# The order of 48 attention blocks in a four-layer graph network: batches in lanes of four, or staggered by three blocks with the last layer's pieces spread out

## The chip, the cores and the metric

The kernel runs on one core of one Trainium2 chip. The metric is device time in microseconds (us) from start to end of the program. Before the change three runs took 4299.87, 4303.16 and 4289.3 us, median 4299.87. The profiled execution spans 4307.9 us.

The engines go by their names in the profile: PE (TensorE, matrix products), PEld (its weight loads), DVE (VectorE), ACT (ScalarE), POOL (GpSimd), SP (SyncE, which here issues transfers).

## What is computed

Sixteen batches of 1024 nodes with 128 features pass four graph layers, all in float32, over one adjacency matrix of 1024 x 1024 that all batches share. The first three layers are attention with 8 heads of 16, then a feed-forward part; the fourth is a graph attention whose scores are a sum of two terms per node.

```python
# layers 0, 1, 2
Q, K, V = h @ Wq, h @ Wk, h @ Wv               # 8 heads of 16
scores = einsum('bnhd,bmhd->bhnm', Q, K) / 4
scores = where(adj == 0, -inf, scores)
attn_out = einsum('bhnm,bmhd->bnhd', softmax(scores), V)
x = layer_norm(h + (attn_out @ Wo + bo))
x = layer_norm(x + relu(x @ W1 + b1) @ W2 + b2)
# layer 3
h = x @ W
e = leaky_relu((h @ a_src)[:, :, None] + (h @ a_dst)[:, None, :], 0.2)
e = where(adj == 0, -inf, e)
y = einsum('bij,bjd->bid', softmax(e), h) + x
out = layer_norm(y)
```

## The kernel before

A block is the attention of one batch b in one layer l of the first three: 48 blocks. A block is 32 steps: two groups of four heads (g), two halves of the queries (qh), eight tiles of the keys (kt). Each step issues the scores, and the product with V of the step four earlier. What lies around the attention (projections of the next block, the feed-forward part of the block before, the fourth layer) is cut into pieces, and at most one piece that is due follows each step. TensorE's order of instructions is the order of this program; the other engines' order is chosen when the kernel is compiled, by priority.

```python
AHEAD = 4
BOTH_ON_DVE = (2, 5, 7)
TILES = {"w": 10, "x": LANES + 1, "last": 2}     # LANES = 4

def slot(dtype=F32):                              # two banks of PSUM each
    return psum.tile([P, N], dtype, tag="s", name="s", bufs=3)
def bank():
    return psum.tile([P, 512], F32, tag="t", name="t", bufs=1)
def e_tile():
    return work.tile([P, J, 512], F32, tag="e", name="e", bufs=6)

def score_step(step):
    ...
    for pp in range(2):                           # two heads each
        ps = slot()
        for r in range(2):
            nc.tensor.matmul(ps[...], k[...], q[...], start=True, stop=True)          # L390
        on_pool = pp == 0 and kt not in BOTH_ON_DVE
        if on_pool:
            nc.scalar.activation(ev, psv, AF.Exp, scale=HD ** -0.5)                   # L397
            nc.gpsimd.tensor_mul(ev, ev, m)                                           # L398
        else:
            nc.vector.tensor_add(ev, psv, m)                                          # L400
            nc.scalar.activation(ev, ev, AF.Exp, scale=HD ** -0.5)                    # L401
    return e

def av_step(step, e, acc, first, last):
    for j in range(J):
        nc.tensor.matmul(acc[...], v_bufs[...], e[:, j, :], start=first, stop=last)   # L407
```

A projection is eight pieces: two transposed halves of x (t0, L260), two products each for keys and queries (L352, split by ACT and DVE into two parts, L354 and L355), two halves of V (L279). What follows a block ("post") is eleven: `both` (transposes on DVE), two out-projections (L279), two transposed halves (`x1t`, L260), four ffn1 (L461), two ffn2 (L279); out-projection and ffn2 are each followed by sums and statistics on DVE and `normalise` on POOL. Each piece of the chain uses the one bank `t`.

The fourth layer of a batch is a chain of 15 pieces:

```python
def edges(u):                       # a quarter of the queries; 2 x 8 matmuls with 4 rows
    def run():
        e = s["e", u] = e_tile()...
        for c in range(2):
            ps = slot()
            ... nc.tensor.matmul(ps[...], h_rows[row, ...], g_rows[row, ...])         # L564
            nc.vector.scalar_tensor_tensor(e[:, c:NT:2, :], ps, 1.0, mask01[...],
                                           op0=OP.max, op1=OP.mult)                   # L567
def aggregate(u):                   # that quarter times the nodes' features
    def run():
        e, ps = s["e", u], bank()
        ... nc.tensor.matmul(ps[...], e[...], s["hd"][...])                           # L576
        ... # reciprocal, sum with x, statistics on DVE; every second: normalise on POOL
def end():                          # scale and shift on POOL, both halves to the output
    ...
# (steps to wait since the piece before, piece, buffers taken and given back)
return [(5, xt(0), "+w +last +w +w"), (1, xt(1), "+w"), (2, nodes(0, 3), ""), (2, nodes(3, 6), ""), (2, nodes(6, 8), "-w -w"),
        (2, rows_gh, ""), (8, edges(0), ""), (2, edges(1), ""), (1, aggregate(0), ""),
        (2, edges(2), ""), (1, aggregate(1), ""), (2, edges(3), ""), (1, aggregate(2), ""),
        (2, aggregate(3), ""), (4, end, "-x -last -w -w")]

blocks = [(b, l) for p in range(0, B, LANES) for l in range(L) for b in range(p, p + LANES)]
```

The scheduler takes the first chain whose next piece is due. `need` takes the pieces of a chain at once, due or not, when the next block cannot do without them:

```python
def piece():
    for chain in chains:
        if now[0] >= chain["due"] + chain["queue"][0][0] and take(chain):
            return
...
if at == 6:                         # step 6 of block m
    need(("post",) + (blocks[m + 1][0], blocks[m + 1][1] - 1) if blocks[m + 1][1] else
         ("fetch", blocks[m + 1][0]))
    put(proj_tasks(m + 1), ("proj", m + 1), first=True)
```

Of the kernel before, what the change touches and what calls it, by code (L numbers as in the profile page):

```python
# [18 lines left out]
P = 128  # L19
H = 8  # L20
HD = 16
# [5 lines left out]
FLOOR = -1e29  # L27
NEG_SLOPE = 0.2
SOON = 120
LANES = 4  # L30
AHEAD = 4
BOTH_ON_DVE = (2, 5, 7)
TILES = {"w": 10, "x": LANES + 1, "last": 2}
BLOCKED = -57344.0


# [70 lines left out]
def fast_path(ctx: ExitStack, tc: tile.TileContext, a: dict, out: bass.AP, flag):  # L107
    nc = tc.nc
    x_dram, adj = a["x"], a["adj"]
    B, N, D = x_dram.shape  # L110
    NT = N // P
    NH = N // 512
    L = 3
# [15 lines left out]
    def half_tile(name):  # L129

        return work.tile([P, 512], F32, tag="w", name=name, bufs=TILES["w"])

# [4 lines left out]
    def load_x(b):  # L137
        t = work.tile([P, NT, D], F32, tag="x", name="x", bufs=TILES["x"])
        nc.sync.dma_start(t, x_dram[b].rearrange("(t p) d -> p t d", p=P))
        return t  # L140

    assert B % LANES == 0 and NT == 8 and D == H * HD == P and N == 2 * 512
    state = {("x", 0): load_x(0)}
    W = [load_layer(nc, nc.sync, const, a, 0, ("Wq", "Wk"))]
    W[0].update(load_layer(nc, nc.scalar, const, a, 0, ("Wv", "bo")))
# [352 lines left out]
    def last_tasks(b):  # L498
# [3 lines left out]
        def xt(h):  # L502
            def run():
                w = W[L - 1]
                if h == 0:

                    s["col"] = work.tile([P, 4, NT], F32, tag="col", name="col", bufs=2)
                    s["hd"] = [work.tile([P, 4, D + 1], F32, tag="w", name="hd", bufs=TILES["w"]) for _ in range(2)]
                    s["n"] = with_stats(state["x", b])
                s["xT", h] = transpose_half("xT", state["x", b], h, w["ln2_gc"], w["ln2_bc"])  # L510
                if h == 1:
                    scale_shift(state["x", b], w["ln2_g"], ln2_b_last)
            return run

        def nodes(t0, t1):
            def run():
                col, ts = s["col"], slice(t0, t1)

                halves = [slice(max(t0, 4 * h), min(t1, 4 * h + 4)) for h in range(2)]
                halves = [(c, s["hd"][c.start // 4][:, c.start % 4:(c.stop - 1) % 4 + 1, :])  # L520
                          for c in halves if c.start < c.stop]
                ps = bank()
                for t in range(t0, t1):
                    nc.tensor.matmul(ps[:, (t - t0) * (D + 2):(t - t0 + 1) * (D + 2)],
                                     s["xT", t // 4][:, t % 4 * P:(t % 4 + 1) * P], w_nodes, start=True, stop=True)
                pv = ps[:, :(t1 - t0) * (D + 2)].rearrange("p (t d) -> p t d", d=D + 2)
                with soon():
                    nc.scalar.activation(col[:, 2, ts], pv[:, :, D + 1], AF.Exp, scale=NEG_SLOPE)
                    nc.scalar.activation(col[:, 0:2, ts].rearrange("p c t -> p t c"), pv[:, :, D:], AF.Exp,
                                         scale=1 - NEG_SLOPE)  # L530
                    for c, hd in halves:
                        nc.vector.tensor_mul(hd[:, :, :D], pv[:, c.start - t0:c.stop - t0, :D],
                                             col[:, 2, c, None].to_broadcast([P, c.stop - c.start, D]))
                for c, hd in halves:
                    nc.scalar.copy(hd[:, :, D], col[:, 2, c])
            return run
# [18 lines left out]
        def edges(u):  # L555
            def run():
                e = s["e", u] = e_tile().rearrange("p j (c q) -> p (j c) q", q=256)
                for c in range(2):

                    ps = slot()  # L560
                    for i in range(2):
                        for r in range(2):
                            row = slice(64 * r + g0, 64 * r + g0 + 4)
                            nc.tensor.matmul(ps[:, (2 * r + i) * 256:(2 * r + i + 1) * 256],  # L564
                                             h_rows[row, (2 * i + c) * P:(2 * i + c + 1) * P],
                                             g_rows[row, u * 256:(u + 1) * 256], start=True, stop=True)
                    nc.vector.scalar_tensor_tensor(e[:, c:NT:2, :], ps.rearrange("p (j q) -> p j q", q=256), 1.0,  # L567
                                                   mask01[:, c:NT:2, u * 256:(u + 1) * 256], op0=OP.max, op1=OP.mult)
            return run
# [21 lines left out]
        def end():  # L591
            y = s["n"][0]
            for h in range(2):
# [1 line left out]
                queue = nc.scalar if h and b == B - 1 else nc.sync  # L595
                queue.dma_start(out[b].rearrange("(t p) d -> p t d", p=P)[:, 4 * h:4 * h + 4], y[:, 4 * h:4 * h + 4, :])

        return [(5, xt(0), "+w +last +w +w"), (1, xt(1), "+w"), (2, nodes(0, 3), ""), (2, nodes(3, 6), ""), (2, nodes(6, 8), "-w -w"),
                (2, rows_gh, ""), (8, edges(0), ""), (2, edges(1), ""), (1, aggregate(0), ""),
                (2, edges(2), ""), (1, aggregate(1), ""), (2, edges(3), ""), (1, aggregate(2), ""),  # L600
                (2, aggregate(3), ""), (4, end, "-x -last -w -w")]

    blocks = [(b, l) for p in range(0, B, LANES) for l in range(L) for b in range(p, p + LANES)]
    chains = []
    done = {("fetch", b) for b in range(2)}
    now = [0]
    free = dict(TILES)  # L610
    free["x"] -= 2
# [361 lines left out]
```

## Time and profile before

| What | Value |
|---|---|
| median of three runs | 4299.87 us |
| span of the profiled execution | 4307.9 us |
| mean granted TensorE clock | 0.974 |
| blocks 4 to 15, 345.9 to 1406.5 us | 1060.6 us |
| blocks 16 to 27, 1406.5 to 2468.0 us | 1061.5 us |
| blocks 28 to 39, 2468.0 to 3523.2 us | 1055.2 us |

The page gives for each engine its busy time, then the span in 40 slices (a digit is the busy share in tenths), then groups of instructions by source line with their mean length. The view by stretches gives the busy time of each engine between two times, with the count of instructions in brackets, then the granted clock of TensorE (1.00 is full), the transfers' share and rate. The view in order of time gives start, length, engine, source line, operation and tiles, how many instructions are merged, and in square brackets how long the engine had been idle and whose result ended that. A busy PE is not PE at its peak: lengths of matmuls overlap, so here the time from start to start counts.

### The profile page before, as it was taken

Reading aid. Unit: us, or ns where it says so; the run is one execution under the profiler, and the core shown is the slowest. Engines: PE = TensorE matmul, PEld = TensorE weight load, DVE = VectorE, ACT = ScalarE, POOL = GpSimd, SP = SyncE. Lnnn points to the kernel's source line nnn. Section 1 sums busy time; section 2 is a strip of 40 time slices with the busy share of each in tenths; the row PEclk is TensorE's granted clock in tenths of the full one; section 3 lists DMA queues with packets and bytes.
Section 4 is the critical chain, followed back from the end, with each engine's and each line's share of the span. In section 5 each row is a group of like instructions: output and inputs, shape, how many; then the busy total and the mean of one; then the engine's idle time right before and its main releaser. Section 6 shows DMA issues by size and latency. Waiting matters only on the chain. (4 is left out here: it accounts for less than half of the span.)

```text
span 4307.9 us, 70734 instructions
## 1 busy us (share of the span) xinstructions
PE 4005.4 (93%) x26069; PEld 1631.7 (38%) x26069; DVE 3408.0 (79%) x5324; ACT 3408.3 (79%) x3961; POOL 3442.0 (80%) x3010
## 2 busy tenths in 40 slices
PE   7999999999999999999999999999999999999996
PEld 2333333344443333334444333333344433333445
DVE  6888878877777888877777787887777788888774
ACT  7898989866767988987676898997776689898660
POOL 4788888876779888887677988887777788888784
PEclk9999999999999999999999999999999999999997
DMA  5222122221111222121112222221211212221100
GB/s 145 64 60 54 49 57 59 58 52 50 43 50 47 60 59 52 49 58 50 50 43 57 56 51 53 60 59 40 60 46 45 64 40 60 59 55 44 45 21 17
DMA packets 126147, 230.77 MB, mean 54 GB/s; under 512 B 36705, under 2 KB 75617, under 8 KB 125793
## 3 DMA queue, kind: packets, MB, share of 16 engines
q1 hardware_dynamic: 122896, 225.14, 20.9%
q8 instruction: 209, 3.42, 0.3%
q10 hardware_dynamic: 2896, 1.01, 0.1%
q14 instruction: 146, 1.19, 0.1%
HBM read 15.54 MB, written 8.39 MB: 6 GB/s over the span
## 5 line engine op out<-in xcount | busy, mean ns | idle before, releaser
L400 DVE TENSOR_TENSOR e<-s,mask_add 128x1024 f32<-128x1024 f32 x2112 | 2503.1, 1212 | 505.6 <-PE s L390 393.0
L401 ACT ACTIVATE e<-e 128x1024 f32<-128x1024 f32 x2112 | 2194.4, 1060 | 428.9 <-DVE e L400 415.3
L398 POOL TENSOR_TENSOR e<-e,mask 128x1024 f32<-128x1024 f32 x960 | 2047.3, 2145 | 470.2 <-ACT e L397 454.2
L407 PE MATMUL acc<-e,v 128*17 128x512 f32 x12288 | 1645.0, 607 | 44.9 <-POOL e L398 32.0
L390 PE MATMUL s<-Wq,Wk 64*128 64x512 f32 x6144 | 1217.0, 461 | 126.5 <-ACT e L397 54.8
L397 ACT ACTIVATE e<-s 128x1024 f32<-128x1024 f32 x960 | 979.8, 1021 | 137.8 <-PE s L390 73.6
L390 PEld LDWEIGHTS s<-Wq,Wk 64*128 64x128 f32 x6144 | 500.6, 186 | 1036.9 <-DVE e L400 330.9
L407 PEld LDWEIGHTS acc<-e,v 128*17 128x17 f32 x12288 | 206.5, 95 | 559.7 <-issue 440.6
L310 POOL TENSOR_SCALAR x<-x,mv 128x128 f32<-128x128 f32 x896 | 389.2, 447 | 22.7
L314 POOL TENSOR_TENSOR x<-x,ln_g 128x1024 f32<-128x1024 f32 (+1 forms) x97 | 228.8, 2359 | 129.8 <-PE t L260 118.9
L576 PEld LDWEIGHTS t<-hd,e 128*128 128x128 f32 x2048 | 259.3, 208 | 67.2 <-issue 31.8
L576 PE MATMUL t<-hd,e 128*128 128x129 f32 x2048 | 271.4, 295 | 7.8 <-DVE x L582 3.5
L308 POOL TENSOR_TENSOR mv<-mv,half_neg 128x4 f32<-128x4 f32 x224 | 232.0, 1036 | 18.3
L298 DVE TENSOR_TENSOR x<-t,x 128x512 f32<-128x512 f32 x192 | 132.1, 688 | 123.3 <-PE t L279 118.9
L461 PE MATMUL t<-x1T,W 128*128 128x512 f32 x384 | 217.7, 649 | 5.1 <-DVE x L582 1.0
L279 PEld LDWEIGHTS t<-W,hT 128*128 128x128 f32 x1536 | 183.9, 196 | 88.0 <-ACT hT L463 35.8
L279 PE MATMUL t<-W,hT 128*128 128x128 f32 x1536 | 202.5, 286 | 3.4 <-DVE lo L355 2.4
L291 DVE BATCH_NORM_STATS2 st<-x 128x6 f32<-128x128 f32 x896 | 197.3, 279 | 2.7
L260 PE MATMUL t<-identf,x 128*128 128x128 f32 x896 | 151.8, 294 | 36.5 <-DVE lo L355 25.5
L260 PEld LDWEIGHTS t<-identf,x 128*128 128x128 f32 x896 | 97.1, 144 | 230.7 <-DVE lo L355 55.8
L306 POOL TENSOR_SCALAR mv<-mv 128x4 f32<-128x4 f32 x224 | 52.8, 236 | 140.0 <-DVE mv L293 101.8
L463 ACT ACTIVATE hT<-t,b 128x512 f32<-128x512 f32 x192 | 132.2, 688 | 40.8 <-PE t L461 40.0
(83 smaller groups left out, 2588.0 us busy)
## 6 DMA issues: line engine op xcount, KB each, us to landing
Wk<-hi SPq DMA_DIRECT2D x384, 128.0 KB
Wk<-lo SPq DMA_DIRECT2D x384, 128.0 KB
Wq<-hi SPq DMA_DIRECT2D x384, 128.0 KB
Wq<-lo SPq DMA_DIRECT2D x384, 128.0 KB
x<-in_x_dram SPq DMA_DIRECT2D x16, 512.0 KB
out_dram<-x SPq DMA_DIRECT2D x31, 256.0 KB
ai<-in_adj_dram SPq DMA_DIRECT2D x8, 512.0 KB
g_rows<-parts SPq DMA_DIRECT2D x124, 4.0 KB
```

The costliest lines, as they stand in the source:

```text
L260: nc.tensor.transpose(ps[:, t * P:(t + 1) * P], src[:, 4 * h + t, :], identf)
L279: nc.tensor.matmul(ps[:, t * P:(t + 1) * P], lhs[f][:, t * P:(t + 1) * P], rhs[f], start=(f == 0), stop=(f == len(lhs) - 1))
L308: nc.gpsimd.tensor_tensor(v, v, half_neg[:, ts], OP.pow)
L310: nc.gpsimd.tensor_scalar(z[:, t, :], z[:, t, :], mv[:, t, 0:1], mv[:, t, 1:2], op0=OP.add, op1=OP.mult)
L314: nc.gpsimd.tensor_mul(z, z, rows(gain, n))
L390: nc.tensor.matmul(ps[:, r * 512:(r + 1) * 512], k[64 * r:64 * r + 64, kt * P:(kt + 1) * P], q[64 * r:64 * r + 64, q0:q0 + 512], start=Tru ...
L397: nc.scalar.activation(ev, psv, AF.Exp, scale=HD ** -0.5)
L398: nc.gpsimd.tensor_mul(ev, ev, m)
L400: nc.vector.tensor_add(ev, psv, m)
L401: nc.scalar.activation(ev, ev, AF.Exp, scale=HD ** -0.5)
L407: nc.tensor.matmul(acc[j * SLOT:j * SLOT + HD + 1, :], v_bufs[m % 2][:, kt, 2 * j + g, :], e[:, j, :], start=first, stop=last)
L576: nc.tensor.matmul(ps[:, i * (D + 1):(i + 1) * (D + 1)], e[:, t, i * P:(i + 1) * P], s["hd"][t // 4][:, t % 4, :], start=(t == 0), stop=(t ...
```

## The change

Before, four batches go together: layer 0 of all four, layer 1 of all four, layer 2 of all four. So the fourth layers of four batches come due within some seven blocks, and the next five blocks have none. After, every third block begins a batch, whose layers 0, 1 and 2 are four blocks apart; the order in between is (b, 0), (b - 1, 1), (b - 2, 2). Batches 2 and 3 begin earlier to fill the start. Each fourth layer can then be spread over the three blocks until the next one: for all but the last four batches each edges piece is followed by its aggregate two steps later, and the next edges piece comes 16 steps after that. The count of buffers is the same.

```diff
-LANES = 4
-TILES = {"w": 10, "x": LANES + 1, "last": 2}
+TILES = {"w": 10, "x": 5, "last": 2}
...
-        return [(5, xt(0), "+w +last +w +w"), (1, xt(1), "+w"), (2, nodes(0, 3), ""), (2, nodes(3, 6), ""), (2, nodes(6, 8), "-w -w"),
-                (2, rows_gh, ""), (8, edges(0), ""), (2, edges(1), ""), (1, aggregate(0), ""),
-                (2, edges(2), ""), (1, aggregate(1), ""), (2, edges(3), ""), (1, aggregate(2), ""),
-                (2, aggregate(3), ""), (4, end, "-x -last -w -w")]
-    blocks = [(b, l) for p in range(0, B, LANES) for l in range(L) for b in range(p, p + LANES)]
+        wide = b < B - 4
+        tasks = [(5, xt(0), "+w +last +w +w"), (1, xt(1), "+w"), (3, nodes(0, 3), ""), (3, nodes(3, 6), ""),
+                 (3, nodes(6, 8), "-w -w"), (2, rows_gh, "")]
+        if wide:
+            for u in range(4):
+                tasks += [(16 if u else 10, edges(u), ""), (2, aggregate(u), "")]
+        else:
+            tasks += [(8, edges(0), ""), (2, edges(1), ""), (1, aggregate(0), ""), (2, edges(2), ""),
+                      (1, aggregate(1), ""), (2, edges(3), ""), (1, aggregate(2), ""), (2, aggregate(3), "")]
+        return tasks + [(4, end, "-x -last -w -w")]
+    early = {(2, 0): 3.5, (3, 0): 7.5}
+    blocks = sorted(((b, l) for b in range(B) for l in range(L)), key=lambda x: early.get(x, 3 * x[0] + 4 * x[1]))
```

More of the change, by code (lines that the diff above doesn't have):

```diff
@@ L140, in load_x @@
         return t
-    assert B % LANES == 0 and NT == 8 and D == H * HD == P and N == 2 * 512
+    assert B >= 4 and NT == 8 and D == H * HD == P and N == 2 * 512
     state = {("x", 0): load_x(0)}
```

## The prediction

> **What bounds the kernel now.** I read the page's busy times and its 40 slices first, then cut the span into the 48 blocks (a new block is 128 score matmuls further on), then looked at single steps.
>
> ```profile
> PE 4005.4 (93%) x26069; PEld 1631.7 (38%) x26069; DVE 3408.0 (79%) x5324; ACT 3408.3 (79%) x3961; POOL 3442.0 (80%) x3010
> ACT  7898989866767988987676898997776689898660
> PEclk9999999999999999999999999999999999999997
> ```
>
> TensorE is far ahead of the others on average; the ACT row breathes with the period of four batches (9s where only attention runs, 6s and 7s where the fourth layer is mixed in). The busy shares by stretch show the two regimes: a plain block (5,1), and a block that carries a fourth layer (5,0).
>
> ```profile
> core 0: us, PE busy (x) PEld busy (x) DVE busy (x) ACT busy (x) POOL busy (x), PEclk, DMA share, GB/s
> 1561.10:1638.90 77.80, 74.09 (x486) 26.43 (x482) 65.34 (x97) 70.05 (x80) 67.10 (x57) 1.00 0.22 55
> 1103.90:1213.30 109.40, 99.79 (x658) 47.44 (x657) 80.26 (x139) 71.39 (x89) 77.08 (x71) 0.94 0.19 49
> ```
>
> Plain: PE 74.1 of 77.8, ACT 70.1. Mixed: PE 99.8 of 109.4, DVE only 73%, ACT 65%. So PE is the nearest to full in both, and the others have room in both. How much of PE's busy time is real need shows where it runs without a wait, in the order of time:
>
> ```profile
> start us, us, engine line op out<-in xcount [idle before <-releaser]
> 1604.39 0.73 PE L390 MATMUL s<-Wq,Wk 64*128 64x512 f32 x4
> 1605.06 1.05 PE L407 MATMUL acc<-e,v 128*17 128x512 f32 x8
> 1606.04 1.16 PE L279 MATMUL t<-Wv,xT 128*128 128x128 f32 x8
> 1607.13 0.73 PE L390 MATMUL s<-Wq,Wk 64*128 64x512 f32 x4
> ```
>
> From start to start: scores 0.67, attention times V 0.98 to 0.99, a projection half 1.09. A step without a piece is 1.645 us. In the same way, from other unhindered steps: a transposed half (L260 x4) 0.59, a 512-column product (L461 or L352 x2) 1.06, ffn2 (L279 x16) 1.98, three node columns (L524 x6) 0.87, an edges piece (L564 x8) about 1.03, an aggregate (L576 x32) 3.775.
>
> Need of PE per block: 32 x 1.645 = 52.6; projections 2 x 0.59 + 4 x 1.06 + 2 x 1.09 = 7.6; post 2 x 1.09 + 2 x 0.59 + 4 x 1.06 + 2 x 1.98 = 11.6; together 71.8 us. A fourth layer: 2 x 0.59 + 2.3 + 0.2 + 4 x 1.03 + 4 x 3.775 = 22.9 us per batch. A plain block lasts 77.5, so it waits 5.7: about 3.2 in the steps without pieces (there DVE and ACT set the pace), about 2.5 where two pieces follow each other and the single bank `t` waits for DVE. Twelve blocks (four batches) from 345.9 to 1406.5 last 1060.6; their need is 12 x 71.8 + 4 x 22.9 = 953.2. So only 107 us, 8.9 per block, are anything but PE's own work, and 5.7 of those 8.9 are in plain blocks too.
>
> **Where the rest goes in mixed blocks.** The chain of order around an edges piece:
>
> ```profile
> 867.62 0.77 PE L564 MATMUL s<-g_rows,h_rows 4*128 4x256 f32 x8
> 869.03 0.50 PE L390 MATMUL s<-Wq,Wk 64*128 64x512 f32 x2 [0.63 <-DVE e L400]
> 870.16 0.56 PE L390 MATMUL s<-Wq,Wk 64*128 64x512 f32 x2 [0.63 <-DVE e L567]
> 870.65 1.91 PE L407 MATMUL acc<-e,v 128*17 128x512 f32 x8
> 872.48 4.49 PE L576 MATMUL t<-hd,e 128*128 128x129 f32 x32
> ```
>
> Edges takes two of the three score slots and 2 x 1.2 us of DVE (L567, 1205 ns), and PE waits twice for DVE. After that L407 takes 1.91 instead of 1.05: the clock is halved.
>
> ```profile
> core 0: us, PE busy (x), PEclk, DMA share, GB/s
> 867.10:870.50 3.40, 2.14 (x20) 0.99 0.00 0
> 870.50:873.90 3.40, 3.40 (x16) 0.50 0.00 0
> ```
>
> I compared all stretches of 3.41 us of the clock records: those in which matmuls other than the 4-row edges ones cover at most 0.54 of the time are followed by half clock, those over 0.58 are not. Of the 48 edges pieces before the last block, 27 are followed by such a stretch. The clock shares of blocks 9 to 15 give 5.1 + 1.7 + 5.1 + 6.8 + 3.4 + 1.7 = 23.8 us lost per four batches, 6.0 per batch. The third loss is GpSimd, when scale-and-shift, normalise and the end piece meet:
>
> ```profile
> 1202.90 1.91 PE L407 MATMUL acc<-e,v 128*17 128x512 f32 x8 [4.00 <-POOL e L398]
> ```
>
> [...]
>
> **The change part by part.** Nothing is removed: the same pieces, so the need stays 953.2 per four batches. What moves: (1) I walked the new order and gaps through the scheduler's code, piece by piece (for the old order that gives the trace's sequence). From block 15 to 42 three kinds of block repeat, with need 80.3 (two aggregates, one edges, end), 76.4 (nodes, one edges, one aggregate, four of post's pieces pushed out) and 81.6 (two edges, one aggregate, double ffn2): mean 79.4.
> (2) Waits of each kind, from the same pieces' waits in the old trace. First kind: block start 0.9, `t` bank 0.9 + 1.2, edges 0.8, aggregates 0.3, free end 1.0 less 0.2, and GpSimd 3.0, because the aggregate's normalise (3.3), x1's scale-shift (4.7), the end piece (5.1) and two normalises (6.6) all fall in steps 19 to 28: 7.9. Second kind 7.0 (the old block 11, alike, had 6.2). Third kind 6.0. Sum 20.9.
> (3) Half clock: four edges pieces per batch as before, 56% of them at about 1.9 us: 4.2, down from 6.0.
> So three blocks take 238.3 + 20.9 + 4.2 = 263.4, twelve 1053.6, against 1060.6, 1061.5 and 1055.2 before. Over 28 such blocks that is -13 us.
> (4) Freed: the two edges tiles held at once (waits of ACT and DVE for L407, 60 + 42 us in all) are now one; these engines are not the bound, so I count nothing.
> (5) The end: batch 15's second layer is now two blocks, not four, ahead of its third, so all 11 pieces of its post are forced in one row at step 6 of block 46. Down that chain each product waits for the one bank and for ACT or DVE, and once for GpSimd's normalise (3.2): some 25 us, 11.6 of it need: +15.
> (6) Tail: block 47 and what follows took 205 us; batch 13's three last aggregates and 13 us of mixed work leave it, but they filled gaps in a chain of latencies: -5 net after the work is counted where it went.
> Sum: 4300 - 13 + 15 - 5 = 4297. My waits are summed one by one, and pieces that fill formerly free steps hide some of them (over the first twelve blocks DVE, ACT and POOL are busy 848.7, 850.3 and 858.9 of 1060.6, a fifth of room); 1 us less per block over the 28 is the correction I choose: 4270.
>
> **Rivals.** (a) Interleaving works: PE's waits in free steps (3.2 per block) vanish because every block has about five more pieces, and edges no longer meet edges. For it: DVE and ACT are idle a quarter of the mixed blocks. Then waits with the half clock fall from 8.9 to 5.5 per block, about 110 us over the 33 blocks from 11 to 43: 4190. Against it: edges waits come from slots and DVE in the very step, not from neighbours. (b) The half clock spreads: edges alone, with wide gaps, in blocks that had clock 1.00; first edges of a batch in the old trace were hit as often as later ones. At 75% hits and 6.83 us stretches it is 8 per batch, +45: 4330. (c) GpSimd becomes a local bound in the first kind: 6 instead of 3 us, +28, about 4310.
>
> **Range and chances.** One us per block is 33 us; I trust the waits to 1.2 us per block, so 40 us, and the end to 15 us. 8 in 10: 4200 to 4335. Faster by over 2% means under 4214: 0.18. Slower by over 2%, over 4386: 0.04. Within: 0.78.
>
> **What would show it.** Blocks in the middle all near 86 to 88 us with PE busy 93 to 95%; the ACT row flat at 7 or 8; the clock's mean near 0.975, its dips one per two edges and spread over the whole span; PE waiting for POOL's L398 once in three blocks; a gap of some 15 us in block 46. I am wrong if the middle blocks last under 84 (rival a), if the mean clock leaves 0.97 to 0.98, or if block 46 costs over 30 us.

## The result, and the profile after

| | before | after |
|---|---|---|
| median of four runs, us | 4301.51 (4289.3 to 4308.17) | 4363.77 (4362.34 to 4372.53) |
| span of the profiled execution, us | 4307.9 | 4370.6 |
| mean granted TensorE clock | 0.974 | 0.972 |

The changed kernel takes 1.0152 times as long, with a 95% interval of 1.0125 to 1.0179. The prediction, 4270 us in a range of 4200 to 4335, is missed by 94 us, on the slow side. From here on spans of the profiled executions are taken apart; their difference, 62.7 us, agrees with that of the medians, 62.3.

The page of the kernel after, busy times and ACT's row of the 40 slices:

```profile
PE 4011.6 (92%) x26069; PEld 1618.1 (37%) x26069; DVE 3402.5 (78%) x5324; ACT 3405.3 (78%) x3961; POOL 3443.5 (79%) x3010
...
ACT  7898988777878777787877878788787877868670
```

The count of PE's instructions is the same 26069, and ACT's row is as flat as the change meant it to be: 7 and 8 from the sixth slice to the thirty-fifth. The work is spread, and the kernel is slower all the same.

Three blocks in a row from the middle, (8,0), (7,1) and (6,2), in the view by stretches of the kernel after:

```profile
1814.10:1902.90 88.80, 83.75 (x556) 34.43 (x552) 70.22 (x115) 69.74 (x78) 70.23 (x61) 0.98 0.22 55
1902.90:1989.40 86.50, 80.48 (x519) 29.96 (x515) 68.87 (x94) 72.42 (x92) 68.87 (x49) 0.98 0.21 52
1989.40:2083.70 94.30, 86.34 (x563) 35.65 (x562) 72.50 (x125) 70.22 (x79) 75.78 (x79) 0.96 0.19 48
```

The first number after the times is the length, the last but two the clock. With the needs that the prediction gave to the three kinds (80.3, 76.4, 81.6), 8.5, 10.1 and 12.7 us of these blocks are something else. The whole kernel can be cut in the same way. For each stretch I count PE's pieces in the trace, price each at its length from start to start (the prediction's own figures), take half of the time that the clock records show at half speed as "half clock", and call the rest "wait". (Where PE also waits inside a stretch at half speed, this counts some wait as half clock. In blocks 16 to 39 of the two kernels that is under 2 us; in block 46 after the change it is 4 of the 17.1, behind it some 10 of the 30.)

| stretch | need before, after | wait + half clock before | after |
|---|---|---|---|
| blocks 0 to 15 | 1232.4, 1209.5 | 143.4 + 30.7 = 174.1 | 132.5 + 22.1 = 154.6 |
| blocks 16 to 39 | 1906.6, 1906.6 | 165.7 + 44.4 = 210.1 | 195.3 + 44.4 = 239.7 |
| blocks 40 to 45 | 432.0, 477.8 | 33.7 + 0 = 33.7 | 47.8 + 6.8 = 54.6 |
| block 46 | 88.3, 93.5 | 8.3 + 6.8 = 15.1 | 18.9 + 17.1 = 36.0 |
| block 47 and what follows | 153.9, 125.8 | 32.5 + 29.1 = 61.6 | 42.4 + 30.1 = 72.5 |
| sum | 3813.2, 3813.2 | 383.6 + 111.0 = 494.6 | 436.9 + 120.5 = 557.4 |

The need is the same to a tenth; the change adds 53 us of wait and 9.5 of half clock. The gain at the start (19.5) and the loss in blocks 40 to 45 (20.9) go with the work of the fourth layers: 22.9 us of need have left the start, and 45.8 have come to blocks 40 to 45. What remains is **the middle, 30 us; block 46, 21; the tail, 11.**

How sure are these two columns? The mean clock is on record for every execution, so its half clock can be had as span x (1 - clock), to some 2 us. In 43 executions of the kernel before this is 94 to 116 us, mean 105, while the remainder of the span stays between 4188 and 4197: what differs from one execution to the next is the half clock. In the four of the kernel after it is 109 to 122, mean 113, and the remainder 4248 to 4252. The two that are taken apart here lie at the upper end, with 111 and 121. So a wait can be compared from one trace to another; a difference of half clock under some 20 us needs the other executions too.

**The middle.** Which waits these are, the view of what PE waits for says directly. Columns: the waiting operation's tile and line, what it waits for, us in total, times, longest. Blocks 16 to 39 before, then after (line numbers are one lower there: L389 is scores, L406 attention times V, L259 a transposed half, L278 out-projection, V or ffn2, L523 and L539 the fourth layer's nodes):

```profile
PE s L390 <- ACT e L397: 27.1, 57, 1.4
PE s L390 <- DVE e L400: 20.0, 32, 1.7
PE acc L407 <- POOL e L398: 20.0, 15, 4.0
PE t L279 <- DVE lo L355: 15.2, 22, 1.0
PE s L390 <- DVE e L567: 15.2, 22, 1.2
PE t L260 <- DVE lo L355: 12.2, 16, 1.0
```

```profile
PE t L278 <- DVE lo L354: 21.0, 24, 1.4
PE t L259 <- DVE x L297: 19.5, 8, 2.5
PE s L389 <- DVE e L566: 19.0, 32, 0.6
PE acc L406 <- POOL e L397: 17.0, 10, 2.1
PE s L389 <- DVE e L399: 15.2, 40, 0.5
PE s L389 <- ACT e L396: 14.1, 32, 0.5
```

Scores waited 62.3 us (27.1 + 20.0 + 15.2) and now wait 48.3: filling free steps does hide waits, 14 us of them. But pieces that wait for the bank `t` until DVE has split a projection (`lo`) go from 30.9 us (15.2 + 12.2, and 3.5 below the lines shown) to 45.9 (21.0 shown, and below the lines shown L523 with 8.8, L259 with 8.6 and L539 with 7.5): a node piece now stands between two projection products, where the bank is still full. And one group is new: eight times 2.4 us for `x L297`, once in every third block. GpSimd's own group hardly shrinks; it is in one place per three blocks now.

**The new wait, step 7 of the third kind.** PE, GpSimd and DVE of the kernel after, in order of time:

```profile
2011.53 0.66 PE L259 MATMUL t<-identf,x 128*128 128x128 f32 x4 [2.44 <-DVE x L297]
```

```profile
2002.26 1.74 POOL L309 TENSOR_SCALAR x<-x,mv 128x128 f32<-128x128 f32 x4
2003.96 4.24 POOL L397 TENSOR_TENSOR e<-e,mask 128x1024 f32<-128x1024 f32 x2
2008.16 0.61 POOL L420 TENSOR_TENSOR A<-tt,recs 128x256 f32<-128x256 f32 x1
```

```profile
2008.81 0.71 DVE L433 STREAM_TRANSPOSE aT<-A 128x512 f32<-128x512 f32 x1 [2.85 <-POOL A L420]
```

The ffn2 pieces of (8,0)'s post are pushed over the block's edge into steps 0 and 1. Their two normalises (L309, the second is shown) land on GpSimd just where it should make masks; it makes two masks, then `A`, the attention output divided by its sums. DVE, idle for 2.85 us, transposes it (aT), and only after that adds `x` to the out-projection (L297, at 2010.79), which frees the bank. The wait is followed by half clock: the attention product at 2013.09 takes 1.80, not 1.05.

**GpSimd, step 26 of the first kind.** GpSimd and PE of the kernel after:

```profile
1876.86 1.29 POOL L313 TENSOR_TENSOR x<-x,ln_gamma 128x512 f32<-128x512 f32 x1
...
1881.93 2.37 POOL L314 TENSOR_TENSOR x<-x,b 128x1024 f32<-128x1024 f32 x1
```

```profile
1886.44 1.45 PE L406 MATMUL acc<-e,v 128*17 128x512 f32 x8 [1.76 <-POOL e L397]
```

The end piece's scale and shift (`ln_gamma`, `ln_beta`) meets the scale and shift of x1 (`ln_g`, `b`); no mask is made from 1873.2 to 1884.2, and PE waits 1.76. Half clock follows: the next ffn1 takes 2.08, unhindered 1.06 to 1.12.

**Block 46.** Two of the eleven pieces in one row, the transposed halves, kernel after:

```profile
4064.05 1.76 PE L259 MATMUL t<-identf,x 128*128 128x128 f32 x4 [1.41 <-POOL x L309]
4067.61 1.76 PE L259 MATMUL t<-identf,x 128*128 128x128 f32 x4 [1.80 <-POOL x L309]
```

The whole row goes from 4057.8 to 4088.2, 30.4 us for 11.6 of need. A wait stands before every one of its ten products, 0.8 us at the least, 2.1 at the most; and all but the last run at half clock (a transposed half unhindered is 0.59 to 0.66, here 1.76). The waits in brackets sum to 10.9; the other 7.9 of the 18.8 us over the need are the slower clock.

### The profile page after: what moved, and what is told of

The parts are those of the page before. It is cut to its first block, busy times and chain, and to the rows that moved or that the text cites. A ratio compares the mean times of both kernels' runs of the same rounds, so it can differ in the third digit from the quotient of the medians.

```text
span 4370.6 us, 70636 instructions
## 1 busy us (share of the span) xinstructions
PE 4011.6 (92%) x26069; PEld 1618.1 (37%) x26069; DVE 3402.5 (78%) x5324; ACT 3405.3 (78%) x3961; POOL 3443.5 (79%) x3010
## 3 DMA queue, kind: packets, MB, share of 16 engines
q10 hardware_dynamic: 2896, 1.01, 0.1%
## 5 line engine op out<-in xcount | busy, mean ns | idle before, releaser
L397 POOL TENSOR_TENSOR e<-e,mask 128x1024 f32<-128x1024 f32 x960 | 2046.3, 2144 | 567.9 <-ACT e L396 565.9
L406 PE MATMUL acc<-e,v 128*17 128x512 f32 x12288 | 1645.9, 608 | 49.1 <-POOL e L397 27.9
L389 PE MATMUL s<-Wq,Wk 64*128 64x512 f32 x6144 | 1216.1, 461 | 108.8 <-ACT e L396 34.8
L389 PEld LDWEIGHTS s<-Wq,Wk 64*128 64x128 f32 x6144 | 500.8, 187 | 1031.9 <-DVE e L399 357.4
L406 PEld LDWEIGHTS acc<-e,v 128*17 128x17 f32 x12288 | 206.9, 96 | 567.4 <-issue 447.7
L309 POOL TENSOR_SCALAR x<-x,mv 128x128 f32<-128x128 f32 x896 | 389.2, 448 | 24.0
L313 POOL TENSOR_TENSOR x<-x,ln_g 128x1024 f32<-128x1024 f32 x97 | 228.7, 2357 | 46.7 <-PE t L259 39.6
L575 PEld LDWEIGHTS t<-hd,e 128*128 128x128 f32 x2048 | 240.2, 195 | 55.9 <-issue 19.7
L575 PE MATMUL t<-hd,e 128*128 128x129 f32 x2048 | 252.4, 282 | 3.2 <-DVE x L581 1.7
L297 DVE TENSOR_TENSOR x<-t,x 128x512 f32<-128x512 f32 x192 | 132.3, 689 | 152.0 <-PE t L278 146.1
L460 PE MATMUL t<-x1T,W 128*128 128x512 f32 x384 | 236.7, 701 | 5.9 <-ACT hT L462 3.1
L278 PEld LDWEIGHTS t<-W,hT 128*128 128x128 f32 x1536 | 183.0, 195 | 86.3 <-ACT hT L462 41.2
L259 PE MATMUL t<-identf,x 128*128 128x128 f32 x896 | 157.6, 297 | 59.9 <-DVE x L297 22.8
L278 PE MATMUL t<-W,hT 128*128 128x128 f32 x1536 | 201.4, 286 | 4.0 <-ACT hT L462 2.3
L290 DVE BATCH_NORM_STATS2 st<-x 128x6 f32<-128x128 f32 x896 | 196.2, 278 | 2.7
L259 PEld LDWEIGHTS t<-identf,x 128*128 128x128 f32 x896 | 98.6, 145 | 259.9 <-DVE x L297 50.9
```

The lines of the kernel that those rows point to most:

```text
L259: nc.tensor.transpose(ps[:, t * P:(t + 1) * P], src[:, 4 * h + t, :], identf)
L278: nc.tensor.matmul(ps[:, t * P:(t + 1) * P], lhs[f][:, t * P:(t + 1) * P], rhs[f], start=(f == 0), stop=(f == len(lhs) - 1))
L309: nc.gpsimd.tensor_scalar(z[:, t, :], z[:, t, :], mv[:, t, 0:1], mv[:, t, 1:2], op0=OP.add, op1=OP.mult)
L389: nc.tensor.matmul(ps[:, r * 512:(r + 1) * 512], k[64 * r:64 * r + 64, kt * P:(kt + 1) * P], q[64 * r:64 * r + 64, q0:q0 + 512], start=Tru ...
L406: nc.tensor.matmul(acc[j * SLOT:j * SLOT + HD + 1, :], v_bufs[m % 2][:, kt, 2 * j + g, :], e[:, j, :], start=first, stop=last)
L460: nc.tensor.matmul(ps, w["W1"][:, f * P:(f + 1) * P], s["x1T", h], start=True, stop=True)
```

## The experiments

Each expectation is quoted as it was written before the run. The time is the median, the ratio is to the kernel before on the same chip, with its 95% interval. "Middle" is wait + half clock of blocks 16 to 39, whose need is 1906.6 in every kernel but one (e15_early, 1907.8; the expectations price it at 1916 and so speak of 230 and 200 us for after and before); before has 165.7 + 44.4, after 195.3 + 44.4. Edits are to the kernel after, where nothing else is said.

**Order alone.** The new order with the old, dense gaps of the fourth layer:

```diff
-        wide = b < B - 4
+        wide = False
```

> The new order of blocks, with the old dense gaps for every batch. If the spreading of the edges pieces is what costs (they meet the half clock and the bank of the projections more often), the three-block cycle falls from 269 to about 264 us and the kernel takes about 4315. If the place of the other pieces costs (feed-forward pieces pushed into the next block, the end piece beside the scale-shift), it stays, since the dense pieces push them too: 4350 to 4380. The forced row in block 46 is the same in both.

4350.93 us, 1.0128 (1.0111 to 1.0145). Middle 187.4 + 25.6 = 213.0, against 210.1 before: without the spread, the staggered order leaves the middle's sum as it was, with more wait and less half clock. Its loss is the end: 52.5 in blocks 40 to 45, 34.8 in block 46, 72.6 after it, much as after. So in these two executions 27 of the 30 us of the middle belong to the spread, and the end to the order. That is an upper end: this execution was the fastest of its four, that of after the slowest, and over all executions the spread costs 10 to 13 us in all (ratio 1.0152 against 1.0128, median 4363.77 against 4350.93), the order some 50 of the 62. The waits of the middle are surer. With the dense gaps the scores wait 73.8 us (48.3 with the spread), the waits for the masks (L397) are 1.5 (17.0), those for `x L297` nil (19.5), those for `lo` 42.4 (45.9). The spread hides 25 us of the scores' waits and pays 35 on the two paths over GpSimd that are shown above; most of the added waits for `lo` came with the order.

**The forced row.** Batch 15's first layer two places earlier and its second one, so that the second is three blocks ahead of the third:

```diff
-    early = {(2, 0): 3.5, (3, 0): 7.5}
+    early = {(2, 0): 3.5, (3, 0): 7.5, (15, 0): 42.5, (15, 1): 46.5}
```

> The kernel after, but batch 15 begins two blocks earlier, so that its layers stand three blocks apart and no row of eleven pieces is forced in block 46. If the forced row and the cold clock behind it cost what block 46 shows (35.6 us of waits and half clock against 14.9 before), the kernel falls by 20 to 25 us, to about 4340. If the row's work only moved (a tail with more left to do), it stays at 4355 to 4370.

4350.63 us, 1.0123 (1.0104 to 1.0143). Block 46 has 5.6 + 0 of wait and half clock instead of 18.9 + 17.1: the row was worth 30.4. But 16 of it come back in the middle (204.7 + 51.2), most of it for a reason that is the experiment's own, in block 39:

```profile
3465.10 1.09 PE L259 MATMUL t<-identf,x 128*128 128x128 f32 x4 [12.00 <-DMA x<-in_x_dram]
```

Batch 15's input is now wanted too soon after its buffer comes free.

**Order of the pieces.** A piece of the fourth layer only when no other piece is due:

```diff
+    def only_last(chain):
+        mark = chain["queue"][-1][3]
+        return mark is not None and mark[0] == "last" and len(chain["queue"]) <= 15
...
-        for chain in chains:
+        for chain in sorted(chains, key=only_last):
```

> The kernel after, but a piece of the fourth layer is taken only when no piece of a feed-forward chain is due. If the pushed ffn2 pieces are a cause (block (6,2) waits 2.4 us for the out-projection's addition on VectorE, which waits for GpSimd, and the half clock follows), the cycle of three blocks loses 4 to 7 us and the kernel 40 to 65: about 4310. If the half clock behind edges alone is the cause, it changes by less than 15 us.

4387.02 us, 1.021 (1.0193 to 1.0227). The waits of the middle fall to 168.6, the level of before: post's pieces are no longer pushed over the edge of the block and node pieces leave the projections alone, though step 7 of the first kind now waits 1.7. The half clock rises to 54.6 (146 us in all over four executions, 113 in after), and in block 11 PE waits 11.7 us for a batch's input (blocks 0 to 15: 181.8 instead of 154.6). So these waits come from the places; mending the places alone does not mend the total.

**No fourth-layer piece in steps 9 to 18**, where the projections are (`only_last` as in the run before):

```diff
+            if only_last(chain) and 9 <= now[0] % 32 <= 18 and now[0] < 32 * len(blocks):
+                continue
```

> The kernel after, but no piece of the fourth layer is taken in steps 9 to 18 of a block, where the products of the next block's projections lie. If pieces between two such products wait for the single bank t (0.8 to 1.1 us each in the second kind: steps 10, 12, 14, 16), the waits of the second kind fall from 8.4 to about 6, and the cycle by 2 to 3 us: 4335 to 4345. If the waits only move to where the pieces go, it stays within 10 us of 4364.

4375.5 us, 1.0185 (1.0154 to 1.0216). Middle 179.1 + 47.8: 16 us of wait less. This is not the price of the node pieces alone: the waits for `lo` fall from 45.9 to 24.6 and those for `x L297` (19.5) go, while PE waits 39.0 instead of 17.0 for the masks and 66.2 instead of 48.3 at the scores. What is kept back lands elsewhere: 12.7 us more than after in blocks 0 to 15, and twelve aggregates instead of eight after block 46 (78.5 there, with 28.8 in block 46 itself).

**The end piece's share of GpSimd.** The last scale and shift is left out (gains are ones and shifts zeros in these inputs, but it is work left out: 5.1 us of GpSimd per batch):

```diff
-                scale_shift(y[:, 4 * h:4 * h + 4, :], wl["ln_gamma"], wl["ln_beta"])
```

> The kernel after without the last layer's scale and shift on GpSimd (5.1 us per batch left out, the gain being all ones and the shift all zeros in this data). If the end piece and x1's scale and shift, one behind the other on GpSimd, hold up TensorE in the first kind of block (1.8 us and the half clock behind it, 1.7), the cycle of three loses about 3.4 us, the kernel 35 to 50 us: about 4320. If GpSimd's load there is hidden, it stays within 10 us of 4364.

4326.24 us, 1.006 (1.004 to 1.008). Middle 180.0 + 25.6: 15 us of wait and 19 of half clock less. PE's waits for the masks (L397) in blocks 16 to 39 go from 17.0 to this:

```profile
PE acc L406 <- POOL e L397: 1.4, 8, 0.2
```

In this pair of executions more than half of what the meeting on GpSimd costs comes as half clock. Over all executions, and the whole span, it is less: the half clock falls by 15 us (113 to 99), the remainder of the span by 25 (4250 to 4225).

**Edges in halves**, two steps instead of one, so that one score slot is taken at a time:

```diff
-                tasks += [(16 if u else 10, edges(u), ""), (2, aggregate(u), "")]
+                tasks += [(16 if u else 10, edges(u, (0,)), ""), (1, edges(u, (1,)), ""), (1, aggregate(u), "")]
```

> The kernel after, but each edges piece of the first twelve batches is taken in two halves, one score slot and one VectorE operation each, in two steps after one another. If the two slots and 2.4 us of VectorE in one step are what stops TensorE and starts the half clock, the waits for L566 and the half-clock stretches behind edges go: 5 to 8 us per batch, the kernel at about 4280 to 4310. If VectorE's work is the cost wherever it lies, it stays within 15 us of 4364.

4345.88 us, 1.0118 (1.0099 to 1.0136). Middle 197.3 + 18.8. Edges pieces that half clock follows: 2 of 52 instead of 20; waits stay.

**Full matmuls added to edges.** Each edges piece gets four transposes of 128 x 128 whose result is never read; this is 0.59 us of added work per piece, 38 us in all 64:

```diff
                     ps = slot()
+                    for k in range(4 if c else 0):
+                        nc.tensor.transpose(ps[:, k * P:(k + 1) * P], w_nodes[:, :D], identf)
```

> The kernel after, with four more 128x128 transposes per edges piece, written into the second score slot ahead of the piece's own matmuls and never read: extra work of TensorE of 0.59 us, 64 times, 38 us. If the half clock comes from a 3.41 us stretch with too few matmuls of full height, the added ones lift such a stretch from 0.43 to 0.60 and the half clock behind edges goes: of 87.8 us lost in the first 47 blocks some 35 go, and the kernel stays within 20 us of 4364 though it does more. If the half clock comes from something else in an edges step (the wait itself), nothing goes and the kernel takes about 4395.

4350.03 us, 1.012 (1.0092 to 1.0148). Middle 196.0 + 27.3, where the added 19 us are counted as wait: they fit into time in which PE waited anyway, and 17 us of half clock go. Edges pieces that half clock follows: 9 of 52. The border that the prediction read from the trace of before (half clock up to 0.54 of a stretch covered, none over 0.58) does not carry over. It was not sharp in the trace of before: there a stretch covered to 0.547 (at 49 us) is followed by half clock, and one covered to 0.525 (at 4240 us) is not. Counted in the same way, both outcomes occur between 0.51 and 0.58 in the trace of after, and eight stretches with added transposes are covered to 0.606 to 0.609 here, and seven of them are followed by half clock.

**The same two, in the order of before.** To the kernel before, edges in halves, each quarter followed at once by its aggregate (all batches; then the first 13), and the added transposes in the first 13 batches:

```diff
-                    for k in range(4 if c else 0):
+                    for k in range(4 if c and b < 13 else 0):
```

> The kernel before, with its order and its bunched fourth layers, but each edges piece in two halves, one score slot each, followed by its aggregate. If the double piece causes the half clock in the mixed blocks (23.8 us of four batches), most of it goes: 15 to 20 us per four batches, the kernel at 4225 to 4250, faster than both. If bunching itself is the cause, it stays within 15 us of 4300.

> The kernel before, with halved edges pieces for batches 0 to 12 alone, the last three whole as they were. If the loss of the run with all batches halved lay only behind block 47 (264 us there against 216), the gain up to block 47 (15 us) now remains: 4280 to 4290. If halving costs elsewhere too, it stays at 4300 or above.

> The kernel before, with the four added transposes of 0.59 us in the edges pieces of batches 0 to 12 (52 times, 31 us of added work). If half clock follows a stretch with too few full matmuls and the transposes fill time in which TensorE waits anyway, half clock in blocks 8 to 39 falls from 68 us to 25 to 40 and the kernel is faster in spite of more work: 4265 to 4290. If the added work is not hidden, 4300 to 4325.

| | median, us | ratio | middle | after block 46 |
|---|---|---|---|---|
| before_split | 4343.39 | 1.0105 (1.0077 to 1.0133) | 179.4 + 27.3 | 106.6 |
| before_split12 | 4312.37 | 1.0027 (1.0015 to 1.004) | 180.6 + 25.6 | 80.7 |
| before_warm12 | 4259.77 | 0.9909 (0.9892 to 0.9925) | 167.1 + 15.4 | 57.4 |

Halves trade half clock for wait, and hurt the end, where the fourth layers are all that is left. The added transposes beat both kernels. The page's busy times, and the added transposes of one edges piece (L562) with the scores that follow, in this kernel:

```profile
PE 3988.5 (94%) x26277; PEld 1628.2 (38%) x26277; DVE 3405.0 (80%) x5324; ACT 3407.0 (80%) x3961; POOL 3442.6 (81%) x3010
```

```profile
859.73 0.66 PE L562 MATMUL s<-identf,w_nodes 128*128 128x128 f32 x4
...
861.45 0.49 PE L390 MATMUL s<-Wq,Wk 64*128 64x512 f32 x2 [0.20 <-DVE e L569]
```

208 instructions more, and PE is busy 17 us less than before (3988.5, was 4005.4), since fewer of the others run at half clock: 111.0 us lost to it before, 59.7 now, of the 53.4 by which the span is shorter. Over the executions on record the half clock is 61 us, where the kernel before on that chip has 106, and the remainder of the span 4197, against 4193. The piece that the prediction showed waits 0.63 for DVE, this one 0.20. The 52 x 0.59 = 31 us of added work are counted as wait here, and the waits of the middle are still 167.1, before 165.7: the added work lies in time in which PE waited anyway.

**A tidy spread.** Edges in halves, gaps of 4 and 1 steps (2 between node pieces), no piece in steps 9 to 18, the fourth layer last among those due, batch 15 earlier; and the same with whole edges:

```diff
-                tasks += [(16 if u else 10, edges(u), ""), (2, aggregate(u), "")]
+                tasks += [(4 if u else 8, edges(u, (0,)), ""), (1, edges(u, (1,)), ""), (1, aggregate(u), "")]
...
+            if only_last(chain) and len(chain["queue"]) > 1 and 9 <= now[0] % 32 <= 18 and now[0] < 32 * len(blocks):
+                continue
```

> All that the single runs point to, on the new order: a piece of the fourth layer only when no feed-forward piece is due and not in steps 9 to 18 (the end piece may), the edges pieces of the first twelve batches in halves with short gaps, and batch 15 begun one block earlier so that nothing is forced near the end. If the cost of the kernel after is where its pieces land, blocks 16 to 39, which hold the same work in every version (1916 us of TensorE's need), fall from 230 us of waits and half clock to 165 to 185 (200 before the change), and the kernel to 4270 to 4300. If mixing a fourth layer into every block costs by itself, blocks 16 to 39 stay over 205 us and the kernel over 4315.

> As the run before, but with whole edges pieces followed by their aggregate two steps later. If whole edges bring the half clock wherever they lie, blocks 16 to 39 have 15 to 30 us more of it than with halves, and the kernel takes 4290 to 4320; if place decides, it is within 8 us of the one with halves.

4414.8 us, 1.028 (1.0253 to 1.0307), and 4374.43, 1.0168 (1.0151 to 1.0185). Middle 209.1 + 70.0 and 189.3 + 61.4: the worst of both terms. An aggregate or half of edges at the start of a block meets the same path through GpSimd's `A`, now in two blocks out of three (step 7 of blocks 24 and 25 waits 2.40 and 2.61). Neither expectation of the second run held: with whole pieces the kernel has less half clock than with halves, and takes 40 us less. A free step is not a free place.

**The path through A.** Its product on DVE instead of GpSimd, in four kernels: after, tidy, after with the transposes and batch 15 earlier, and before_warm12:

```diff
-            nc.gpsimd.tensor_mul(state["A"][:, qh, :, g, :], tt[:, :, :HD],
+            nc.vector.tensor_mul(state["A"][:, qh, :, g, :], tt[:, :, :HD],
```

> The kernel after, with the product of the attention and its reciprocal sums (A) on VectorE in place of GpSimd. If the path from a busy GpSimd over A to the out-projection carries the loss, the wait of 2.4 us at step 7 of every third block and the half clock behind it (1.7) go: blocks 16 to 39 fall from 230 to 190 to 205 us of waits and half clock, the kernel to 4325 to 4345. If VectorE's added work (192 times some 0.3 us) sets back the scores as much, it stays at 4355 to 4375.

> The tidy run with A on VectorE. There the wait at step 7 or 10 stands in all three kinds of block (2.5, 2.5 and 3.7 us, each with the half clock behind it). If the path carries it, some 12 us per three blocks go, 100 over the kernel: 4300 to 4325. If the pieces' places cost by themselves, it stays above 4380.

> The kernel after with three mendings: the added transposes against the half clock, batch 15 begun one block earlier, A on VectorE. If the causes add up, 4364 less 14, 15 to 25 and 25 to 35 gives 4290 to 4310: no better than the kernel before without any. If the new order hides something more, it stays over 4320.

> The kernel before with the added transposes, and A on VectorE. If GpSimd's path also costs in the old order (waits of 4.0 us for the masked scores once in four batches, and three forced transposes), it falls from 4260 to 4240 to 4255; if VectorE's added work costs more than that, 4260 to 4275.

| | median, us | ratio | middle |
|---|---|---|---|
| after_A_dve | 4502.55 | 1.0478 (1.0449 to 1.0507) | 237.4 + 47.8 |
| tidy_A_dve | 4513.39 | 1.0499 (1.0465 to 1.0534) | 256.2 + 71.7 |
| after_warm_end_A | 4469.45 | 1.0395 (1.0365 to 1.0424) | 238.8 + 39.2 |
| before_warm12_A | 4418.29 | 1.0287 (1.0254 to 1.0319) | 228.5 + 41.0 |

All lose, in plain blocks too (blocks 17 to 19: 77.5 us before, 80.1 in before_warm12_A, without half clock in either). The product itself shows why; lengths are min, median and max in ns, before and in after_A_dve:

```profile
L421 POOL TENSOR_TENSOR A<-tt,recs x192: 611/622/647, 68.6 to 4200.4; 128x256 f32<-128x256 f32 x192
```

```profile
L420 DVE TENSOR_TENSOR A<-tt,recs x192: 403/1364/6233, 66.2 to 4402.6; 128x256 f32<-128x256 f32 x192
```

On DVE it can take 0.40 (the expectation's "some 0.3 us" was an estimate of mine, which no trace shows), and takes 1.36 in the middle case and up to 6.2. The long ones go with GpSimd's instructions. In after_A_dve 76 of the 192 products take 0.40 to 0.43 us. The other 116 take 0.61 or more; each of them begins while a GpSimd instruction runs, and ends 0.28 to 0.29 us after one has ended. One of them, with GpSimd's instruction:

```profile
158.94 2.39 POOL L313 TENSOR_TENSOR x<-x,ln_g 128x1024 f32<-128x1024 f32 x1 [3.00 <-PE t L259]
159.44 2.17 DVE L420 TENSOR_TENSOR A<-tt,recs 128x256 f32<-128x256 f32 x1
```

GpSimd ends at 161.33, the product at 161.61. What ties the two together, no run here shows. One more thing the run settles: in block 23 the wait at step 7 goes from 2.44 to none with no half clock after it, and the group `x L297` is gone from the waits of the middle. So the path is the one read above. Its worth could not be had this way.

**A sooner on GpSimd.** The product stays there and gets a higher priority:

```diff
+            with soon():
                 nc.vector.reciprocal(rec, tt[:, :, HD])
                 nc.gpsimd.tensor_mul(state["A"][:, qh, :, g, :], tt[:, :, :HD],
```

> The changed kernel, with the reciprocal and GpSimd's product of A put ahead in priority, nothing else. Theory (GpSimd's order makes the wait at step 7 of every third block): about 2.4 us of wait and 1.7 us of half clock go from one block in three; blocks 16 to 39 go from 230 us over their need to about 200, the kernel to 4325 to 4345. Rival (what GpSimd does first is not decided by priority there, or the wait only moves to the masks of the scores): 4355 to 4375.

4400.43 us, 1.0236 (1.0215 to 1.0258). The rival held: in the same place of this kernel GpSimd still makes both masks first,

```profile
2005.94 4.24 POOL L397 TENSOR_TENSOR e<-e,mask 128x1024 f32<-128x1024 f32 x2
2010.15 0.61 POOL L421 TENSOR_TENSOR A<-tt,recs 128x256 f32<-128x256 f32 x1
```

and the wait is 2.44 as before. Elsewhere the order did change: PE waits 22.8 us for the masks in the middle, it was 17.0. But 4400 is outside the rival's 4355 to 4375 too, and how is worth more than the run was meant to tell: the waits of the middle are those of after (196.2, was 195.3), and the half clock is 66.6 instead of 44.4. Of the 27.5 us between the two spans, 23.3 are half clock; over all executions it is 141 to 150 us, against 109 to 122 in after.

**The causes together**: transposes in all edges pieces, batch 15's first two layers one place earlier each (43.5 and 46.5, so that its input isn't late), A sooner:

> The changed kernel with the added transposes in each edges piece of the first thirteen or so batches, batch 15's first two layers two places earlier, and A's product put ahead on GpSimd. Theory: the three causes add up, 4285 to 4320, and the order itself gives nothing, so it stays above the old order with the added transposes alone (4260). Rival: over 4330, and the new order hides another cost.

4326.76 us, 1.0068 (1.0047 to 1.0088), between the two theories' numbers. Middle 197.0 + 27.3; block 46 has 5.6 + 0; blocks 40 to 45 and the tail keep 54.8 and 77.9. The two causes that were taken away are gone (half clock 120.5 to 83.0 in all, block 46 36.0 to 5.6); the waits of the middle were not, since A stayed where it was. Against before_warm12, which has the same transposes in the old order (but for the last three batches: 12 pieces, 7 us), it is 67 us slower, 71 in the spans: 30 of wait and 12 of half clock in the middle, 21 in blocks 40 to 45, 20 in the tail, less 12 in block 46 and the start. So with the half clock behind edges and the forced row treated, the new order is still the slower one.

## Why the prediction was wrong

**Right: that the need stays and sets the level.** It is 3813.2 us before and after, 87% of the span. The signs came in part: ACT's row is flat, the mean clock is 0.972, PE waits for GpSimd's masks once in three blocks; but the third kind of block lasts 94.3, not 86 to 88, and block 46 costs 36.0, over the 30 that were named as a sign of being wrong. Rival (a), that interleaving makes the waits vanish (4190), was wrong for the reason given against it: waits behind edges arise in the very step, and are 19.0 us in the middle, 15.2 before. Rival (b) needed hits of 75%; they are 20 of 52, and the half clock of blocks 16 to 39 is the same 44.4 as before. (Its sum is off too: 0.75 x 4 x 3.41 is 10.2 per batch, not 8. And the plain block shown as (5,1) is (6,1).) Rival (c) put 3 us more per three blocks on GpSimd; its group of waits in the middle is smaller than before (17.0, was 20.0), though no_end_scale shows that it is worth 15 us of wait there.

**Failed: "1 us less per block over the 28 is the correction I choose".** This made 4270 out of 4297. Its mechanism exists: scores wait 14.0 us less over blocks 16 to 39, 0.6 per block. What was left out is that a piece that fills a free step brings its own wait, for the bank `t` (+15.0 for `lo`) and, once in three blocks, for the path GpSimd, DVE, bank (+19.5). The waits alone needed a correction of plus 1.2 per block (195.3 measured, 8 x 20.9 = 167.2 summed, over 24 blocks), not minus 1.

**Failed: "First kind ... 7.9. Second kind 7.0 ... Third kind 6.0. Sum 20.9".** Blocks 21 to 23 have waits of 6.8, 8.4 and 9.3 (length less need less half clock): 24.5. The first kind was priced too high; GpSimd's term there was 1.76, not 3.0. The second was mis-sized by the bank: two node pieces, the product between them and L539 wait 0.77, 1.01, 0.33 and 0.94 for `lo` in block 22. The third was mis-sized by its step 7, which I took from the old trace, where no ffn2 is pushed past the block's end: 2.4.

**Failed: "four edges pieces per batch as before, 56% of them at about 1.9 us: 4.2, down from 6.0".** Measured 44.4 / 8 = 5.6, no less than before. Edges did get hit less often (20 of 52, not 56%), but edges are not the only cause: in blocks 21 to 23 half clock follows the waits of steps 26 (GpSimd) and 7 (`x L297`) as well. From block 2 to block 45 half clock sets in 36 times: 20 times after a stretch of 3.41 us with an edges piece, 16 times after one without (before, 27 and 6). The prediction had counted the stretches that come before half clock, and priced those with edges alone.

**Failed: "some 25 us, 11.6 of it need: +15".** The row takes 30.4, and block 46 is 26.1 longer than before (129.5, was 103.4), 5.2 of it need. The term that was missed is the clock. The waits of the row, 10.9, are within the 13.4 that the prediction's 25 less 11.6 allowed; 7.9 us of slower clock in the row come on top, and were not in the sum.

**Failed: "-5 net" of the tail.** The need did leave (28.1), the waits grew by 9.9 instead. The clearest of them is in the last chain of the kernel after:

```profile
4333.92 0.55 PE L563 MATMUL s<-g_rows,h_rows 4*128 4x256 f32 x1 [7.16 <-DMA h_rows<-parts]
```

Before, PE waited 2.2 there, with other work to do. The prediction itself said that batch 13's aggregates "filled gaps in a chain of latencies", and still counted a gain.

The sum of the terms, as waits and half clock in the two spans: the middle 239.7 measured against 8 x 25.1 = 200.8 (+39), block 46 +20.9 for the +15 forecast (+6), the tail +10.9 for -5 (+16), start and blocks 40 to 45 together +1.4. That is 62 of the 67 us between 4297 and 4363.8; the choice of 1 us per block adds the other 27.

**What stays open.** Where in GpSimd's order A goes is not settled by the priority that I changed, so the worth of the path (some 2.4 us and the half clock behind it, once in three blocks) was seen in single blocks and not in a total. The added waits for `lo` were read from the view of waits, and no run removed them alone. And the half clock of a given version could not be predicted from its waits: after_A_soon against after.

## What to carry to other kernels

Whether interleaving regimes pays where another engine is the fullest in each, no run here shows. Where it is the same engine, as here, the pieces keep their need, and a new place for a piece is worth only the waits of that place: price each by what holds its bank and by what the engine ahead of it does first (here GpSimd made two masks, 4.24 us, and then `A`). Forcing a chain of pieces through one bank in a row cost its latencies and then its clock (10.9 and 7.9 us in block 46). Full matmuls added where PE waited anyway made a kernel here faster with more work (before_warm12: 31 us added, 42 us less time); look at the clock's row before and after, not at the count of instructions.

## What the hardware showed that I had not expected

- Unread transposes made the kernel before faster: 31 us of added matmuls, 51 us less half clock in the two traces (45 in the mean of the executions), 42 us less time (0.9909, 0.9892 to 0.9925). In after, edges pieces that half clock follows are 20 of 52, with the added transposes (edges_warm) 9 of 52. What it is in the added work that keeps the clock, no run here shows.
- The 47 stretches at half clock in the trace of after all begin within 2 ns of one grid of 3.413 us, over the whole span, and 38 of them last 3.413 us.
- Two kernels with the same waits within 1 us (195.3 and 196.2 in blocks 16 to 39) lose 44.4 and 66.6 us to half clock there, and each holds its time within 11 us over four runs. Half clock does not follow from the sum of the waits. What it does follow from, no run here shows.
- A product of 128 x 256 on DVE took 0.40 to 6.2 us in a kernel with a busy GpSimd, 1.36 in the middle case, where GpSimd itself takes a steady 0.62. All 116 products of 0.61 us and more ended 0.28 to 0.29 us after a GpSimd instruction.
